# A graph layer on one core: two steps of twelve gathered chunks in place of four of seven, with completion counters of their own

## The chip, the core and the metric

The kernel runs on one core of a Trainium2 chip. The metric is device time in microseconds (us) of one execution. Fourteen runs of the kernel before have a median of 15300.56 us (15264.44 to 15319.17).

## The reference

A graph has 50,000 nodes with a row of 128 float32 each, and 1,650,000 edges, sorted by destination. An edge has a source, a destination and one of two types. Cut to what matters:

```python
Xs = X[src]
m_data = Xs @ W_data.T + b_data
m_ctrl = Xs @ W_control.T + b_control
msg = jnp.where((edge_types == 0)[:, None], m_data, m_ctrl)
agg = jax.ops.segment_sum(msg, dst, num_segments=X.shape[0])
out = jax.nn.relu(agg + (X @ W_self.T + b_self))
return _layernorm(X + out)
```

Every node has one edge to itself, so 50,000 of the edges are loops.

## The kernel before

The two products with the message weights are linear, so the kernel first sums the source rows per destination and type, and multiplies the sums afterwards. The edge list is cut into blocks: `NBLK` = 435, of which 433 are regular and the first and last are plain. A regular block covers 3,800 edges: `Q` = 4 steps of `R` = 7 chunks of 128 edges, 4 x 22 fillers, and 128 single rows.

**Gathers.** For each of the 28 chunks POOL issues one indirect DMA (line 451) that brings 128 source rows of 512 bytes into a tile `y`, out of a pool of 70. TensorE multiplies it with a one-hot matrix `oh` (line 454) whose columns are the 2 x 38 pairs of type and destination in the step's window. The result `acc` of a step is added by VectorE (DVE) into the block's running sums (`add`, line 465), at a place read into a register.

**Loops and fillers.** A loop edge needs no gather, since a node's own row is near. `fill` (lines 297 to 327) takes the loops out of the chunks, puts fillers (other edges) in their places, and works out which nodes were left out. That is a chain of DVE operations on [128, 28, 22] elements: `m`, `new`, `v_new`, `idx`, `col`, `old`, `by`. It runs `RAHEAD` = 5 blocks ahead. The nodes left out come back through `pl` (lines 344 to 358), which `add_left_out` (line 363) adds to the sums.

**Single rows.** The last 128 edges of a block are fetched by ordinary DMAs of one row each, 64 on SP's queue and 64 on ACT's (`single_rows`, line 439), two blocks ahead (`AHEAD`). In each of the four steps either engine loads 16 addresses into registers with one load (line 434) and issues 16 rows. They form a 29th chunk `yx` of the last step.

**Completion.** The tile framework gives each DMA one of a few completion counters, in turn: eight for POOL's gathers, eight shared by the queues of SP and ACT. Whoever issues on a counter first waits until the DMA before on the same counter has landed. In the built program each gather from the ninth on waits for the gather eight before, and once the 70 buffers are used also for TensorE; and almost every single row waits for an earlier transfer.

**Order.** Instructions go to each engine in the order of the loop from line 520 on (`manual_schedule`). Per block: the last step's `add` of the block before; ACT copies the shifted sums over (`take_over`, line 470); DVE adds the left-out nodes; then for each step `products`, and between them the layer of the block before (`layer`, `moments`, `store`, lines 472 to 498), the one-hot and its column counts two blocks ahead (`onehot` line 396, `counts` lines 406 and 411), `fill`, and `single_rows`. SP also carries the loads of a block's own rows (`window`, lines 387 and 389), the output (line 498) and, every ten blocks, the edge lists. Every ten blocks `columns` (lines 234 to 285) prepares the next ten on DVE.

Of the kernel before, what the change touches and what calls it, by code (L numbers as in the profile page):

```python
# [12 lines left out]
BF16 = mybir.dt.bfloat16  # L13
I32 = mybir.dt.int32
U8 = mybir.dt.uint8
# [8 lines left out]
D = 128  # L24
# [9 lines left out]
R = 7  # L34
W = 38
Q = 4
B = 128
C = R * Q
X = 128
C1 = C + 1  # L40
F = 22
# [9 lines left out]
AHEAD = 2  # L51
RAHEAD = 5
LOOP = 1024.0
# [26 lines left out]
def straight(ctx, tc, c, x, x_t, src_t, dst_t, etype_t, src_f, dst_f, etype_f, src_x, dst_first, first_p, out):  # L80
# [19 lines left out]
    gat = ctx.enter_context(tc.tile_pool(name="gat", bufs=70))  # L100
# [9 lines left out]
    idx0 = keep.tile([P, C], I32, name="idx0")  # L110
    nc.sync.dma_start(idx0, src_t[:, :C])
# [5 lines left out]
    FILL = Q * F + C  # L117
# [108 lines left out]
    def packed(src, col, name):  # L226

        lim = eds.tile(list(col.shape), F32, name="lim" + name, bufs=1)
        nc.vector.tensor_scalar(lim, col, 0.0, float(P - 1), op0=ALU.max, op1=ALU.min)
        v = eds.tile(list(col.shape), F32, name="v" + name)  # L230
        nc.vector.scalar_tensor_tensor(v, src, float(P), lim, op0=ALU.mult, op1=ALU.add)
        return v

    def columns(g):
# [5 lines left out]
        def first_of(rel, d):  # L240
            yield (rel[:, :, :C].rearrange(steps, r=R), d[:, :, :C].rearrange(steps, r=R),
                   first[:, :, :, None].to_broadcast([P, GB, Q, R]))
            yield rel[:, :, C:], d[:, :, C:], first[:, :, Q - 1:]

        def first_of_f(rel, d):
# [4 lines left out]
        h = eds.tile([P, GB, Q, R + 1], BF16, name="h_loop", bufs=1)  # L250
        nc.vector.memset(h, 0.0)
        nc.vector.tensor_tensor(h[:, :, :, :R], a["s"][:, :, :C].rearrange(steps, r=R),
                                a["d"][:, :, :C].rearrange(steps, r=R), op=ALU.is_equal)
        rank = ps_r.tile([P, GB * Q, R + 1], F32, name="rank")
        hs_ = h.rearrange("p b q r -> p (b q) r")
        nc.tensor.matmul(rank, below, hs_, start=True, stop=False)
        for r in range(R):
# [10 lines left out]
        cb = eds.tile([P, GB, C], F32, name="cb")  # L268
        nc.vector.tensor_scalar(cb, a["t"][:, :, :C], 0.0, float(P), op0=ALU.not_equal, op1=ALU.mult)
        nc.vector.tensor_tensor(cb, cb, a["d"][:, :, :C], op=ALU.add)  # L270
        nc.vector.tensor_tensor(cb, cb, base[:, g * GB:(g + 1) * GB, :].to_broadcast([P, GB, C]), op=ALU.subtract)


        rk = eds.tile([P, GB, C], F32, name="rk")
        nc.vector.scalar_tensor_tensor(rk.rearrange(steps, r=R), h[:, :, :, :R], -LOOP,
                                       rank.rearrange("p (b q) r -> p b q r", q=Q)[:, :, :, :R],
                                       op0=ALU.mult, op1=ALU.add)
# [3 lines left out]
        stay = eds.tile([P, GB, C], F32, name="stay")  # L281
        nc.vector.scalar_tensor_tensor(stay, rk, F - LOOP, v[:, :, :C], op0=ALU.is_ge, op1=ALU.mult)
# [14 lines left out]
    def fill(b):  # L297

        if plain(b):
# [6 lines left out]
        m = fil.tile([P, C, F], F32, name="m")  # L306
        nc.vector.tensor_tensor(m, rk_g[g][:, i, :, None].to_broadcast([P, C, F]),  # L307
                                rank_no_ps[:, None, :].to_broadcast([P, C, F]), op=ALU.is_equal)
        new = fil.tile([P, C, F], F32, name="new")
        nc.vector.tensor_tensor(new.rearrange("p (q r) f -> p q r f", r=R), m.rearrange("p (q r) f -> p q r f", r=R),  # L310
                                vf.rearrange("p (q f) -> p q f", f=F)[:, :, None, :].to_broadcast([P, Q, R, F]),
                                op=ALU.mult)
        v = fil.tile([P, C], F32, name="v_new")
        nc.vector.tensor_reduce(v, new, AX.X, ALU.add)  # L314
        vi = fil.tile([P, C], I32, name="vi")
        nc.vector.tensor_tensor(vi, v, stay_g[g][:, i, :], op=ALU.add)
        idx = fil.tile([P, C], I32, name="idx", bufs=RAHEAD + 2)
        nc.vector.tensor_single_scalar(idx, vi, 7, op=ALU.logical_shift_right)
        nc.vector.scalar_tensor_tensor(col_g[g][:, i, :C], idx, -float(P), vi, op0=ALU.mult, op1=ALU.add)
        idxs[b] = idx  # L320

        old = fil.tile([P, C, F], F32, name="old")
        nc.vector.tensor_tensor(old, m, cb[:, :, None].to_broadcast([P, C, F]), op=ALU.mult)
        by = fil.tile([P, Q, F], BF16, name="by")
        with nc.allow_low_precision(reason="whole numbers below 256, one of them not 0"):
            nc.vector.tensor_reduce(by, old.rearrange("p (q r) f -> p q f r", r=R), AX.X, ALU.add)  # L326
# [33 lines left out]
    def add_left_out(b):  # L360
        if not plain(b):
            part = sums[b % RING][:, :, :B]
            nc.vector.tensor_tensor(part, pls.pop(b)[:, :, :B], part, op=ALU.add)  # L363

    def chunks_of(b, q):

        n = C1 if not plain(b) else C if b == 0 else RCH if b < NBLK else 0
        return range(q * R, max(q * R, min((q + 1) * R if q < Q - 1 else C1, n)))

    def steps_of(b):  # L370
        return [q for q in range(Q) if len(chunks_of(b, q))]

    idxs = {0: idx0}
    bys, pcs, zs, pls = {}, {}, {}, {}
    ats = {}
    ohs, cnts, ys, accs, xws, xTs, pos, hs, mvs, sds = {}, {}, {}, {}, {}, {}, {}, {}, {}, {}
# [5 lines left out]
    def window(b):  # L384
        at = base_of(b)
        xw = stp.tile([B, D], F32, name="xw", bufs=5)
        nc.sync.dma_start(xw, x[bass.ds(at, B), :])
        xT = stp.tile([P, B], F32, name="xT", bufs=5)
        nc.sync.dma_start(xT, x_t[:, bass.ds(at, B)])
        xws[b], xTs[b] = xw, xT  # L390

    def onehot(b):
        g, i = divmod(b, GB)
        n = C1 if not plain(b) else C if b == 0 else RCH
        oh = ohp.tile([P, C1, 2 * W], F32, name="oh")
        nc.vector.tensor_tensor(oh[:, :n, :], col_g[g][:, i, :n, None].to_broadcast([P, n, 2 * W]),  # L396
                                num_ps[:, None, :].to_broadcast([P, n, 2 * W]), op=ALU.is_equal)
        ohs[b] = oh

    def counts(b):  # L400

        cnt = ohp.tile([P, Q, 2 * W], BF16, name="cnt")
        with nc.allow_low_precision(reason="whole numbers up to R + 1"):
            whole = [q for q in range(Q) if len(chunks_of(b, q)) == R]
            n = len(whole)
            nc.vector.tensor_reduce(cnt[:, :n, :], ohs[b][:, :n * R, :].rearrange("p (q r) w -> p q w r", r=R),  # L406
                                    AX.X, ALU.add)
            for q in steps_of(b):
                if q not in whole:
                    k = chunks_of(b, q)  # L410
                    nc.vector.tensor_reduce(cnt[:, q, :], ohs[b][:, k[0]:k[-1] + 1, :].rearrange("p r w -> p w r"),  # L411
                                            AX.X, ALU.add)
        cnts[b] = cnt

    SHARE = X // 2
    TURN = SHARE // Q
    RANGE = dict(min_val=0, max_val=(N - 1) * ROW, skip_runtime_bounds_check_because="where a node's row is")
    x_bytes = x.rearrange("n d -> (n d)").bitcast(U8)[None, :]

# [7 lines left out]
    def single_rows(b, q):  # L427

        if q == 0:
            ys[b] = stp.tile([X, D], F32, name="yx", bufs=AHEAD + 2)  # L430
        both = []
        for j, (eng, dma) in enumerate(((SP, nc.sync), (ACT, nc.scalar))):
            at = j * SHARE + q * TURN
            _, rows = nc.values_load_multi_w_load_instructions(  # L434
                ats[b][0:1, at:at + TURN], engines=[eng], **RANGE)
            both.append([(dma, at + k, row) for k, row in enumerate(rows)])
        for pair in zip(*both):
            for dma, k, row in pair:
                dma.dma_start(ys[b][k:k + 1, :].bitcast(U8), x_bytes[:, bass.ds(row, ROW)])  # L439

    def products(b, q):
        g, i = divmod(b, GB)
        acc = ps.tile([P, 3, W], F32, name="acc")
        ks = chunks_of(b, q)
        for k in ks:
            if k == C:
                r, y = X, ys.pop(b)
            else:
                r = LAST if b == NBLK - 1 and k == RCH - 1 else P
                y = gat.tile([P, D], F32, name="y")  # L450
                nc.gpsimd.indirect_dma_start(  # L451
                    out=y[:r], out_offset=None, in_=x,
                    in_offset=bass.IndirectOffsetOnAxis(ap=idxs[b][:r, k:k + 1], axis=0))
            nc.tensor.matmul(acc[:, :2, :].rearrange("p t w -> p (t w)"), y[:r], ohs[b][:r, k, :],  # L454
                             start=k == ks[0], stop=k == ks[-1])
        for t in range(2):
            nc.tensor.matmul(acc[:, 2, :], to_row[:, t, :], cnts[b][:, q, t * W:(t + 1) * W],  # L457
                             start=t == 0, stop=t == 1)
        accs[b, q] = acc
# [7 lines left out]
    def take_over(b):  # L467
        at = nc.values_load(shift_i[0:1, b:b + 1], engines=[ACT], min_val=0, max_val=B,  # L468
                            skip_runtime_bounds_check_because="it was clamped to this")
        nc.scalar.copy(sums[b % RING][:, :, :B], sums[(b - 1) % RING][:, :, bass.ds(at, B)])  # L470
# [10 lines left out]
    def moments(b):  # L481
# [5 lines left out]
        nc.vector.bn_aggr(mv, st)  # L487
        sd = stp.tile([B, 1], F32, name="sd")
        nc.scalar.activation(sd, mv[:, 1:2], AF.Sqrt, bias=c["eps"][:B, :])
        hs[b], mvs[b], sds[b] = h, mv, sd  # L490

    def store(b):
# [5 lines left out]
        nc.sync.dma_start(out[bass.ds(base_of(b), B), :], o)  # L498
# [10 lines left out]
    for b in range(1, RAHEAD):  # L509
# [3 lines left out]
        if b < AHEAD:  # L513
            onehot(b)
            counts(b)
            for q in range(Q):
                single_rows(b, q)
        if b == 1:
            clear_sums()
    for b in range(NBLK + 1):  # L520
# [9 lines left out]
        if b > 0:  # L530
            add(b - 1, steps_of(b - 1)[-1])
            if b < NBLK:
                take_over(b)
        if b < NBLK:
            add_left_out(b)
# [393 lines left out]
```

## Time and profile before

| What | Value |
|---|---|
| median of 14 runs | 15300.56 us |
| the profiled execution: its time, and its span | 15289.41 us, 15287.4 us |
| PE busy | 7318.0 us (48%) |
| DVE busy | 6912.4 us (45%) |
| ACT busy | 353.8 us (2%) |
| POOL busy | 11491.8 us (75%) |
| granted TensorE clock | 1.000 |
| mean share of the 16 DMA engines, and rate | 2 tenths, 63 GB/s |
| DMA issues: gathers, single rows | 12160, 2 x 27712 |

The span runs from the first to the last instruction. Busy time of an engine leaves out the instructions of its sequencer: register loads, semaphore waits and the issue of DMAs on SP and ACT. So ACT, busy for 2%, may still have a full queue. For POOL a gather does count as busy[...]. A row of the groups of instructions gives the count, the busy time and the mean of one, then the engine's idle time just before, and what ended it.

### The profile page before, as it was taken

What the parts mean: (1) busy time and instruction counts of PE and PEld (TensorE: products, weight loads), DVE (VectorE), ACT (ScalarE), POOL (GpSimd) and SP (SyncE); (2) the same over time, 40 slices, a digit from 0 to 9 for tenths busy, and PEclk for the clock granted to TensorE, in tenths of its full rate; (3) what the DMA queues carried; (4) which work ended last, traced back from release to release, by engine and by line L of the source; (5) the groups of instructions that cost most, each with busy time, mean ns of one, the idle gap of its engine ahead of it and who ended that gap; (6) DMA issues with size and microseconds to landing.
All of it is one profiled execution on the core that took longest, in us unless ns stands there. A gap on an engine that the chain in (4) does not pass through costs nothing.

```text
span 15287.4 us, 239078 instructions
## 1 busy us (share of the span) xinstructions
PE 7318.0 (48%) x34233; PEld 6788.6 (44%) x34234; DVE 6912.4 (45%) x12861; ACT 353.8 (2%) x875; POOL 11491.8 (75%) x12170
## 2 busy tenths in 40 slices
PE   4444444444444444445666544444444444444444
PEld 3444444444444444444444444444444444444444
DVE  5444444444444444444444444444444444444443
ACT  0000000000000000000000000000000000000000
POOL 7777777777777777777777777777777777777776
DMA  2222222222222222222222222222222222222221
GB/s 66 63 65 63 63 64 65 63 64 63 63 63 65 63 63 63 65 64 64 63 63 63 64 63 63 63 63 64 63 63 63 63 63 63 63 65 63 63 63 52
DMA packets 724493, 968.72 MB, mean 63 GB/s; under 512 B 282786, under 2 KB 522533, under 8 KB 722896
## 3 DMA queue, kind: packets, MB, share of 16 engines
q0 software_dynamic: 389120, 797.69, 20.0%
q1 hardware_dynamic: 277914, 141.12, 3.4%
q10 hardware_dynamic: 55862, 14.50, 0.4%
q14 instruction: 1314, 10.76, 0.2%
q8 instruction: 283, 4.64, 0.1%
HBM read 923.55 MB, written 28.66 MB: 62 GB/s over the span
## 4 chain that ended last, share of the span: by engine, by line
DMA 42%; ACTq 20%; issue 13%; SPq 10%; PE 8%; DVE 6%; ACT 1%; POOL 0%; DVEq 0%; POOLq 0%
DMA yx<-in_x 34%; ACTq L439 16%; SPq L439 8%; PE acc L454 6%; ACTq L434 3%; DMA y<-in_x,idx 3%; DMA out<-o 2%; DMA xT<-in_x_t 2%; DVE sums L363 1%; ACT sums L470 1%; ACTq L468 1%; DMA xw<-in_x 1%; SPq L381 1%; DMA vf_all<-vd 1%; PE pl L349 1%
## 5 line engine op out<-in xcount | busy, mean ns | idle before, releaser
L451 POOL DMA_INDIRECT y<-in_x,idx x12152 | 11482.7, 945 | 3714.7 <-issue 2017.6
L454 PE MATMUL acc<-oh,y 128*128 128x76 f32 x24320 | 5779.5, 424 | 500.2 <-DMA y<-in_x,idx 492.2
L454 PEld LDWEIGHTS acc<-oh,y 128*128 128x128 f32 x24320 | 5431.4, 330 | 691.3 <-DMA y<-in_x,idx 657.1
L363 DVE TENSOR_TENSOR sums<-pl,sums 128x384 f32<-128x384 f32 x433 | 241.3, 557 | 7740.1 <-ACT sums L470 7740.1
L349 PE MATMUL pl<-z,ones_b 88*128 88x256 bf16 x433 | 170.7, 394 | 4403.4 <-DVE sums L363 4265.9
L349 PEld LDWEIGHTS <-ones_b 88*128 88x128 bf16 x433 | 45.2, 104 | 4452.0 <-DVE sums L363 4451.9
L333 PE MATMUL small<-ones_b,by 128*88 128x1 bf16 x433 | 100.2, 232 | 2812.8 <-DVE by L326 2755.7
L333 PEld LDWEIGHTS <-by 128*88 128x88 bf16 x433 | 64.3, 148 | 2860.6 <-DVE by L326 2860.5
L406 DVE TENSOR_REDUCE cnt<-oh 128x228 bf16<-128x1596 f32 (+2 forms) x435 | 1279.0, 2940 | 0.1
L396 DVE TENSOR_TENSOR oh<-col,small 128x2204 f32<-128x2204 f32 (+2 forms) x435 | 1050.0, 2414 | 0.0
L457 PEld LDWEIGHTS <-to_row 128*128 128x128 bf16 x3476 | 633.3, 194 | 0.0
L326 DVE TENSOR_REDUCE by<-old 128x88 bf16<-128x616 f32 x433 | 577.7, 1334 | 15.0
L470 ACT COPY sums<-sums 128x384 f32 x434 | 222.2, 512 | 14139.0 <-DMA yx<-in_x 13648.5
L478 PE MATMUL po<-wmsgT,sums 128*128 128x128 f32 x1740 | 531.5, 461 | 0.0
L465 DVE TENSOR_TENSOR sums<-acc,sums 128x114 f32 x1738 | 473.9, 273 | 126.3 <-PE acc L457 39.0
L411 DVE TENSOR_REDUCE cnt<-oh 128x76 bf16<-128x608 f32 x434 | 503.6, 1160 | 0.0
L457 PE MATMUL acc<-cnt,to_row 128*128 128x38 bf16 x3476 | 473.6, 220 | 0.0
L478 PEld LDWEIGHTS po<-wmsgT,sums 128*128 128x128 f32 x1740 | 403.3, 322 | 97.5 <-issue 97.5
L310 DVE TENSOR_TENSOR new<-m,small 128x616 f32<-128x616 f32 x433 | 344.3, 795 | 14.8
L307 DVE TENSOR_TENSOR m<-rk,small 128x616 f32<-128x616 f32 x433 | 344.3, 795 | 14.7
L314 DVE TENSOR_REDUCE v_new<-new 128x28 f32<-128x616 f32 x433 | 344.1, 795 | 14.8
L476 PE MATMUL po<-bias,sums 3*128 3x128 f32 x870 | 344.5, 497 | 1.2 <-DVE sums L465 1.2
(116 smaller groups left out, 4068.3 us busy)
## 6 DMA issues: line engine op xcount, KB each, us to landing
yx<-in_x ACTq DMA_DIRECT2D x27712, 0.5 KB
yx<-in_x SPq DMA_DIRECT2D x27712, 0.5 KB
y<-in_x,idx POOLq DMA_INDIRECT x12152
xw<-in_x SPq DMA_DIRECT2D x435, 64.0 KB
xT<-in_x_t SPq DMA_DIRECT2D x435, 64.0 KB
out<-o SPq DMA_DIRECT2D x435, 64.0 KB
vf_all<-vd SPq DMA_DIRECT2D x44, 440.0 KB
s<-in_src_t SPq DMA_DIRECT2D x44, 145.0 KB
```

What stands on the lines that cost most here:

```text
L326: nc.vector.tensor_reduce(by, old.rearrange("p (q r) f -> p q f r", r=R), AX.X, ALU.add)
L363: nc.vector.tensor_tensor(part, pls.pop(b)[:, :, :B], part, op=ALU.add)
L396: nc.vector.tensor_tensor(oh[:, :n, :], col_g[g][:, i, :n, None].to_broadcast([P, n, 2 * W]), num_ps[:, None, :].to_broadcast([P, n, 2 * W ...
L406: nc.vector.tensor_reduce(cnt[:, :n, :], ohs[b][:, :n * R, :].rearrange("p (q r) w -> p q w r", r=R), AX.X, ALU.add)
L411: nc.vector.tensor_reduce(cnt[:, q, :], ohs[b][:, k[0]:k[-1] + 1, :].rearrange("p r w -> p w r"), AX.X, ALU.add)
L434: _, rows = nc.values_load_multi_w_load_instructions(ats[b][0:1, at:at + TURN], engines=[eng], **RANGE)
L439: dma.dma_start(ys[b][k:k + 1, :].bitcast(U8), x_bytes[:, bass.ds(row, ROW)])
L451: nc.gpsimd.indirect_dma_start(out=y[:r], out_offset=None, in_=x, in_offset=bass.IndirectOffsetOnAxis(ap=idxs[b][:r, k:k + 1], axis=0))
L454: nc.tensor.matmul(acc[:, :2, :].rearrange("p t w -> p (t w)"), y[:r], ohs[b][:r, k, :], start=k == ks[0], stop=k == ks[-1])
L457: nc.tensor.matmul(acc[:, 2, :], to_row[:, t, :], cnts[b][:, q, t * W:(t + 1) * W], start=t == 0, stop=t == 1)
L465: nc.vector.tensor_tensor(part, accs.pop((b, q)), part, op=ALU.add)
L478: nc.tensor.matmul(po, a[:, t, :B], c["wmsgT"][:, t * D:(t + 1) * D], start=False, stop=t == 1)
```

## The change

- A step has `R` = 12 chunks and `W` = 60 destinations, a block `Q` = 2 steps, 2 x 42 fillers and 2 x 64 single rows: 3,284 edges, 24 gathers, 128 single rows. `NBLK` is 503. A block's sums have `B` = 112 columns.
- The 64 single rows of a step are a 13th chunk of 64 partitions in each step. `fill`, `columns` and `counts` run over `C1` = 26 chunk columns in place of 28 or 29, with 42 fillers.
- Gathers go in passes of 6 into one tile of 6 x 128 rows, of which there are `SLOTS` = 10. Each slot has a semaphore `landed`; the six gathers of a pass count on it, and TensorE waits once for all six. The framework's counters and their waits are gone from the gathers.
- Single rows count on semaphores `fetched`, one for each queue and each of four buffers. TensorE waits once a block for all 128. The framework's waits between rows are gone. An engine loads 32 addresses at a time, twice a block.
- `take_over` on ACT and `add_left_out` on DVE become one DVE operation, `begin_sums`. The square root stands in a function of its own (`root`), a pass later, and `store` a pass later than before.

```diff
-R = 7
-W = 38
-Q = 4
-B = 128
+R = 12
+W = 60
+Q = 2
+PASS = 6
+B = 112
 C = R * Q
-X = 128
-C1 = C + 1
-F = 22
+F = 42
+S = 64
+X = Q * S
+R1 = R + 1
+C1 = Q * R1
...
+SLOTS = 10
...
-    gat = ctx.enter_context(tc.tile_pool(name="gat", bufs=70))
+    gat = ctx.enter_context(tc.tile_pool(name="gat", bufs=SLOTS))
...
+        with nc.allow_low_precision(reason="whole numbers up to R1"):
+            nc.vector.tensor_reduce(cnt, ohs[b].rearrange("p (q r) w -> p q w r", r=R1), AX.X, ALU.add)
...
         for j, (eng, dma) in enumerate(((SP, nc.sync), (ACT, nc.scalar))):
-            at = j * SHARE + q * TURN
+            at = j * TURN + part * LOAD
             _, rows = nc.values_load_multi_w_load_instructions(
-                ats[b][0:1, at:at + TURN], engines=[eng], **RANGE)
...
-                dma.dma_start(ys[b][k:k + 1, :].bitcast(U8), x_bytes[:, bass.ds(row, ROW)])
...
+            for dma, sem, k, row in pair:
+                copy = dma.dma_start(ys[b][k:k + 1, q, :].bitcast(U8), x_bytes[:, bass.ds(row, ROW)])
+                copy.then_inc(sem, 16)
+                tc.no_tile_sem_insts.add(copy.ins.name)
+                tc.add_to_no_dep_group(f"single{b}", copy.ins)
+
+    def rows_fetched(b):
+
+        times = len(range(b % ROW_SLOTS or ROW_SLOTS, b + 1, ROW_SLOTS))
+        for j in range(2):
+            wait = nc.tensor.wait_ge(fetched[j][b % ROW_SLOTS], 16 * Q * TURN * times)
+        tc.declare_fence(wait.ins, group=f"single{b}")
...
+    def gathers(b, ks):
+        i = pass_no[0] % SLOTS
+        pass_no[0] += 1
+        y = gat.tile([P, PASS, D], F32, name="y")
         for k in ks:
...
+            r = LAST if b == NBLK - 1 and k == RCH - 1 else P
+            copy = nc.gpsimd.indirect_dma_start(
+                out=y[:r, k % PASS, :], out_offset=None, in_=x,
+                in_offset=bass.IndirectOffsetOnAxis(ap=idxs[b][:r, column(k):column(k) + 1], axis=0))
+            copy.then_inc(landed[i], 16)
+            tc.no_tile_sem_insts.add(copy.ins.name)
+            tc.add_to_no_dep_group(f"rows{b}_{ks[0]}", copy.ins)
+        seen[i] += 16 * len(ks)
+        wait = nc.tensor.wait_ge(landed[i], seen[i])
+        tc.declare_fence(wait.ins, group=f"rows{b}_{ks[0]}")
+        return y
...
+    def begin_sums(b):
+
+        part = sums[b % RING][:, :, :B]
+        if b == 0:
+            return
+        at = nc.values_load(shift_i[0:1, b:b + 1], engines=[DVE], min_val=0, max_val=B,
                             skip_runtime_bounds_check_because="it was clamped to this")
-        nc.scalar.copy(sums[b % RING][:, :, :B], sums[(b - 1) % RING][:, :, bass.ds(at, B)])
+        old = sums[(b - 1) % RING][:, :, bass.ds(at, B)]
+        if plain(b):
+            nc.vector.tensor_copy(part, old)
+        else:
+            nc.vector.tensor_tensor(part, pls.pop(b)[:, :, :B], old, op=ALU.add)
...
         if b > 0:
             add(b - 1, steps_of(b - 1)[-1])
-            if b < NBLK:
-                take_over(b)
         if b < NBLK:
-            add_left_out(b)
...
+            begin_sums(b)
+        last = steps_of(b)[-1:]
+        for q, (step, ks) in enumerate(passes_of(b)):
+            if ks:
+                products(b, step, ks)
...
             if q == 1 and b > 0:
+                root(b - 1)
+            if q == 2 and b > 0:
                 store(b - 1)
...
-            if not plain(b + AHEAD):
-                single_rows(b + AHEAD, q)
+            if q % 2 == 0 and not plain(b + AHEAD):
+                single_rows(b + AHEAD, q // 2, 0)
```

## The prediction

> **What bounds the kernel now.** I first read the engines' busy shares and the costliest group, then POOL's waits, then single gathers in the timeline, then the queues of SP and ACT, and last the end of the span. The page:
>
> ```profile
> span 15287.4 us, 239078 instructions
> ...
> L451 POOL DMA_INDIRECT y<-in_x,idx x12152 | 11482.7, 945 | 3714.7 <-issue 2017.6
> ```
>
> POOL's busy share of 75% misleads. A gather costs its 945 ns and the idle time before it: (11482.7 + 3714.7) / 12152 = 1.2506 us. All 12160 gathers take 15207 us, 99.5% of the span. Is the idle part a wait? POOL's waits (total us, times, longest) and the first gathers of the timeline answer:
>
> ```profile
> POOL y L451 <- issue: 2018.8, 6615, 0.3
> POOL y L451 <- PE acc L454: 890.8, 2901, 2.4
> POOL y L451 <- DMA y<-in_x,idx: 453.9, 1486, 0.3
> ```
>
> ```profile
> 9.66 0.94 POOL L451 DMA_INDIRECT y<-in_x,idx  x1 [0.31 <-issue]
> 10.91 0.94 POOL L451 DMA_INDIRECT y<-in_x,idx  x1 [0.30 <-issue]
> 12.16 0.94 POOL L451 DMA_INDIRECT y<-in_x,idx  x1 [0.30 <-issue]
> ```
>
> Whatever is named as the releaser, the gap is 0.30 us (890.8 / 2901 = 0.307). In the built program the second to eighth gather wait for nothing, neither a counter nor a buffer, and they too start 1.25 us apart. So the gap belongs to the gather, and POOL waits for nobody: the kernel is bound by the count of gathers at 1.2506 us each. A regular block has 28, so 35.0 us.
>
> Close behind comes the issue of single rows. ACT's copy (line 470) starts at 5019.50 and 5054.49, again 35.0 us apart, and DVE waits for that copy 7740.1 us in all. A stretch of the chain of waits on ACT (start, length):
>
> ```profile
> 5003.49 1.36 ACTq L434
> ...
> 5005.88 0.23 ACTq L439
> ...
> 5006.22 0.23 ACTq L439
> ...
> 5006.55 0.23 ACTq L439
> ...
> 5007.55 1.62 DMA yx<-in_x
> ```
>
> Free rows start 0.333 us apart; then the queue stands 1.62 us until an earlier row has landed and its counter is free. SP has the same waits:
>
> ```profile
> SPq L439 <- DMA yx<-in_x: 1880.0, 4977, 1.8
> L434 ACTq TENSOR_LOAD <-at_x x1732: 1010/1299/1499, 23.9 to 15228.0; - x193
> L434 SPq TENSOR_LOAD <-at_x x1732: 972/1225/1462, 36.8 to 15223.0; - x193
> ```
>
> That is 1880.0 / 433 = 4.3 us a block on SP, and a load of 16 addresses costs 1.2 to 1.3 us.
>
> At the end POOL's last gather starts at 15214.04, takes 0.99, and the span goes on for 72 us: the copies on ACT and the products are about two blocks behind POOL. The first gather starts at 8.2. So 8.2 + 15207 + 72 = 15287.
>
> **The change, part by part.**
>
> *Gathers.* The built program has 24 + 501 x 24 + 13 = 12061 in place of 12160: 99 x 1.2506 = 124 us less, on the path. The framework's counters go, but as shown they hold nobody up: 0. In their place POOL waits once in six gathers, for TensorE to be done with the pass ten before, 75 us earlier. Behind that wait stand all later gathers. I take 0, as long as the other engines keep to 24 x 1.2506 = 30.0 us a block. That is the condition of the whole forecast, so each engine is summed against 30.0.
>
> *SP.* 64 rows. One costs issue 228 ns, a register move 29 and gaps of about 70, 0.327 us as on ACT: 20.9. Loads of 32 addresses do not occur in the trace. One address costs 0.540 us (line 381), 16 cost 1.225, so 46 ns for each more and 1.96 for 32; bounds are 1.225 (no more than for 16) and 2.45 (twice it). I take 1.96, from two rows of the same form; with 0.1 around each, 4.1 for both. Window and output: one load 0.54, three DMAs of 0.36, 0.36 and 0.38, gaps 0.4: 2.0. Nine issues per ten blocks for the edge lists at 0.45: 0.4. Sum 27.4, between 26.0 and 28.4. The output waits for DVE's `store`, and the second 32 rows are queued behind it; TensorE needs these only two blocks later, so the wait must only leave SP its 27.4 between one `store` and the next.
>
> *ACT.* 64 x 0.333 = 21.3; two loads of 2.08 (0.569 for one address on line 468, 1.299 for 16) and 0.3 for the slower first row after each: 4.8; the root 0.3 and its wait about 0.2. Sum 26.6. The copy of 0.51 and its load of 0.57 leave ACT.
>
> *The waits on rows.* The 4.3 us a block on SP, and some 6 on ACT (35.0 less 26.6 and the copy), go. Do they come back because the transfers are slow? The Trainium skill (DMA: Bandwidth & Descriptors, "Why a DMA increments its semaphore by 16 and not by 1") says that a DMA of one row from SP or ACT runs on the lowest-numbered engine alone, which speaks against this change: 128 rows in 30.0 us on one of 16. The table of queues gives ACT's rows 0.4% of 16 engines' span: 0.004 x 16 x 15287 / 27712 = 35 ns each. By the rule 128 x 35 ns = 4.5 us, with the gathers' 20% beside them about 11 of 30.0; spread evenly it would be 6. Either way there is room. I take 0.
>
> *DVE.* Elementwise operations grow by 1.04 ns an element (2418 ns at 2204, 755 at 608). `m`, `new`, `v_new`, `old` at 26 x 42 = 1092 elements: 795 + 476 x 1.04 = 1290 each, 5.16 us; `oh` at 3120: 3.37. For the column counts three rows give the law:
>
> ```profile
> L411 DVE TENSOR_REDUCE cnt<-oh 128x76 bf16<-128x608 f32 x433 | 503.4, 1163 | 0.0
> L406 DVE TENSOR_REDUCE cnt<-oh 128x304 bf16<-128x2128 f32 x1 | 3.9, 3856 | 0.0
> L406 DVE TENSOR_REDUCE cnt<-oh 128x76 bf16<-128x532 f32 x1 | 1.1, 1078 | 0.0
> ```
>
> With 7 elements an output costs (3856 - 1078) / 228 = 12.2 ns, over a base of 150; an eighth adds 85 / 76 = 1.1. So 13 cost 18.9, times 240 outputs: 4.7 us; by elements alone it would be 5.6. `by`, likewise, 1.84 to 2.25. Two `add` of 0.34, `begin_sums` 0.51, the other small rows of a block unchanged at 3.5, `columns` 7.8 per ten blocks 0.8, three register loads of 0.30 that are partly covered 0.9. Sum 21.5, at most 22.8, against 15.9 busy before. DVE now waits 7740.1 / 433 = 17.9 us a block for ACT's copy; that goes, and next it waits for TensorE's layer after the first pass, within the 8.5 us left over.
>
> *PE.* 26 products of two records each. 14 records of 76 columns take 3.2 us, 0.23 each; line 478 with 128 columns takes 0.30. So at most 52 x 0.30 = 15.6, plus layer 2.8 and small ones 2: 20.4. The wait for six gathers makes the first of them late by 6.3 us; nothing but the order on TensorE hangs on that, and `add` needs the last of a step anyway.
>
> *DVE against POOL.* The Trainium skill (SBUF — State Buffer, "SBUF: two separate sides") warns that while DVE runs certain copies from SBUF to SBUF, POOL cannot write descriptors. The candidates here, `o`, `idx` and `at_x` (0.374 + 0.218 + 0.243 = 0.84 us a block), would by the rule cost up to 433 x 0.84 = 364 us now and 420 after. The row says otherwise: a mean of 945 against 0.94 in the timeline, 12 us in all. I scale that by 503 / 435: +2.
>
> *The tail.* ACT no longer lags. From the last gather: landing about 2 (a row took 1.62), one product and the counts 1.2, `add` 0.8, layer 2.8, moments and root 1.4, `store` 0.6, then the last checks on DVE 2.9 and 13.4 from DVE's end at 15274.0 to the span's: 25. The trace has no such drain; bounds are 20 and the present 72. I take 27, nearer to the sum.
>
> **Sum.** 8.2 + 12061 x 1.2506 + 2 + 27 = 15121. The profiled execution is 2.0 over its span, and the median of the runs is 11.2 over it: 15121 + 13 = 15134 us, 1.1% under 15300.56.
>
> **The rivals.**
>
> *The rows' waits were the queue's own (slower).* If SP or ACT cannot issue 32 rows in a run at 0.33 us, and the 4.3 us come back in another form, SP takes 27.4 + 4.3 = 31.7 a block, POOL stands at its slots, and 501 x 31.7 + 37 before the first row + 60 after the last + 13 gives 15990. It decides from 2.6 us a block on: 40 ns a row, or 1.3 us a load. For it: 32 rows in a run are nowhere in the trace, and SP has 9% of slack. Against it: seven free rows in the chain follow each other without slowing, and a row takes 35 ns of a DMA engine. 9%.
>
> *DVE, or the loop between DVE and TensorE, exceeds 30.0 at times.* `columns` adds 7.8 us in one block of ten; with 8.5 to spare and 60 gathers in buffers I expect no stall. If the spare were 2 and POOL stood 6 us in each of 51 groups: 15134 + 306 = 15440; at half of it 15290. 4%.
>
> *The counters do pace POOL (much faster).* If half the 0.30 were the wait on a counter: 12061 x 1.10 + 48 = 13320. The unwaited gathers speak against it. 3%.
>
> **How the numbers follow.** POOL-bound at the same pace has 84%, and its time is the prediction. Its own range: 10 less at the undisturbed pace of 1.2498, 7 less tail, 11 less if the next median lies at the profile; 45 more with today's tail, 20 more for twice the disturbance: 15095 to 15215. That holds over 8 in 10 and needs no other case. A measurement of this kernel can tell about 0.2% (30 us) from no change. Faster: 84 + 3 = 87%; same: 3 of the DVE case's 4; slower: 9 + 1.
>
> **What would show it.** Right: the gather row at 945 ns with 1.25 us a gather and 12061 of them; no wait of POOL over 0.3 us in the middle of the span; rows on SP and ACT 0.33 us apart without waits; DVE near 70% busy; a tail under 40 us. Wrong: POOL waiting for TensorE for microseconds once a pass, with SP or ACT never idle (first rival) or DVE never idle (second); loads of 32 addresses over 3 us; gathers clearly over 0.95 us.

## The result, and the profile after

The changed kernel takes 15122.34 us (median of 6 runs, 15121.93 to 15125.28) against 15300.28 us for the kernel before (28 runs): ratio 0.9884, interval 0.9874 to 0.9894. The forecast was 15134 us. The profiled execution takes 15124.06 us. But in two of the three later groups of runs, each on a chip of its own, the kernel before took 45% longer and the changed kernel 57 to 59%, so that there the change made the kernel 7.5 to 8.6% slower.

From the page of the changed kernel, its span and three of its groups (busy us, mean ns of one | idle time before):

```profile
span 15122.4 us, 243274 instructions
...
L464 POOL DMA_INDIRECT y<-in_x,idx x12048 | 11393.6, 946 | 3681.9 <-issue 3577.2
...
L409 DVE TENSOR_REDUCE cnt<-oh 128x240 bf16<-128x3120 f32 x503 | 2914.8, 5795 | 0.1
L525 DVE SCALAR_TENSOR_TENSOR h<-po,xw 112x128 f32<-112x128 f32 x503 | 146.6, 291 | 2996.3 <-PE po L520 2942.6
```

A gather costs (11393.6 + 3681.9) / 12048 = 1.2513 us, as before to a thousandth. There are 12061 of them (13 stand in a row of their own). The first starts at 8.6, the last at 15098.7; it takes 1.0, and the span goes on for 22.6 us after its end, where it went on for 72 before. Of the 165 us between the two spans the gathers make up 115 and this tail 50. POOL's waits (total us, times, longest):

```profile
POOL y L464 <- issue: 3581.2, 11733, 0.3
...
POOL y L464 <- PE acc L483: 14.8, 39, 3.2
```

No wait of weight is left, though POOL now has one wait per pass. The condition of the forecast was that the other engines keep to 30.0 us a block. The new loads of 32 addresses (minimum/median/maximum ns), then the wait of SP that is largest in total:

```profile
L435 ACTq TENSOR_LOAD <-at_x x1002: 2121/2154/2474, 21.0 to 15009.8; - x167
L435 SPq TENSOR_LOAD <-at_x x1002: 1866/2077/2257, 33.0 to 15021.1; - x167
```

```profile
SPq L543 <- DVE o L542: 730.9, 335, 27.5
```

All waits of SP together are 1353 us over the whole span, and 2.5 us a block between 1000 and 14000 us: SP works 27.5 of each 30.0 us. ACT's queue, counted in the same way from the trace, works 24.9 and waits 5.1, nearly all for DVE. The waits of a row for an earlier row (1880.0 us before) are gone. DVE is busy 10619.7 us (70%), 21.1 a block, and its largest idle time is the one for TensorE's layer (line 525), 5.9 us a block.

### The profile page after: what moved, and what is told of

Read it like the earlier page. It is cut to its first block, busy times and chain, and to the rows that moved or that the text cites. A ratio compares the mean times of both kernels' runs of the same rounds, so it can differ in the third digit from the quotient of the medians.

```text
span 15122.4 us, 243274 instructions
## 1 busy us (share of the span) xinstructions
PE 8027.3 (53%) x34836; PEld 6859.4 (45%) x34837; DVE 10619.7 (70%) x13316; ACT 151.6 (1%) x509; POOL 11407.5 (75%) x12071
## 3 DMA queue, kind: packets, MB, share of 16 engines
q10 hardware_dynamic: 64566, 16.74, 0.6%
## 4 chain that ended last, share of the span: by engine, by line
POOL 59%; issue 21%; PE 9%; DMA 6%; DVE 5%; PEld 1%; SPq 0%; ACTq 0%; POOLq 0%; PEldq 0%; ACT 0%; DVEq 0%
POOL y L464 59%; DMA y<-in_x,idx 5%; PE acc L483 5%; PE po L520 2%; PE po L518 1%; DVE cnt L409 1%; PE po L517 1%; DVE by L329 0%; PEld acc L483 0%; DVE h L525 0%; SPq L440 0%; DVE st L527 0%; ACTq L440 0%; DVE m L310 0%; DVE new L313 0%
## 5 line engine op out<-in xcount | busy, mean ns | idle before, releaser
L464 POOL DMA_INDIRECT y<-in_x,idx x12048 | 11393.6, 946 | 3681.9 <-issue 3577.2
L483 PE MATMUL acc<-oh,y 128*128 128x120 f32 x24122 | 5749.8, 427 | 6309.0 <-PEq L471 6281.6
L409 DVE TENSOR_REDUCE cnt<-oh 128x240 bf16<-128x3120 f32 x503 | 2914.8, 5795 | 0.1
L401 DVE TENSOR_TENSOR oh<-col,small 128x3120 f32<-128x3120 f32 x503 | 1695.8, 3371 | 0.0
L329 DVE TENSOR_REDUCE by<-old 128x84 bf16<-128x1092 f32 x501 | 1066.9, 2130 | 17.4
L489 PE MATMUL acc<-oh,yx 64*128 64x120 f32 x2004 | 767.3, 484 | 8.2 <-PEq L449 8.2
L310 DVE TENSOR_TENSOR m<-rk,small 128x1092 f32<-128x1092 f32 x501 | 647.1, 1292 | 17.1
L313 DVE TENSOR_TENSOR new<-m,small 128x1092 f32<-128x1092 f32 x501 | 647.0, 1291 | 17.0
L317 DVE TENSOR_REDUCE v_new<-new 128x26 f32<-128x1092 f32 x501 | 646.7, 1291 | 17.0
L326 DVE TENSOR_TENSOR old<-m,small 128x1092 f32<-128x1092 f32 x501 | 642.9, 1283 | 0.0
L520 PE MATMUL po<-wmsgT,sums 128*112 128x128 f32 x2012 | 518.7, 403 | 0.0
```

Source lines behind the costliest of these rows:

```text
L401: nc.vector.tensor_tensor(oh, col_g[g][:, i, :, None].to_broadcast([P, C1, 2 * W]), num_ps[:, None, :].to_broadcast([P, C1, 2 * W]), op=AL ...
L409: nc.vector.tensor_reduce(cnt, ohs[b].rearrange("p (q r) w -> p q w r", r=R1), AX.X, ALU.add)
L464: copy = nc.gpsimd.indirect_dma_start(out=y[:r, k % PASS, :], out_offset=None, in_=x, in_offset=bass.IndirectOffsetOnAxis(ap=idxs[b][:r, c ...
L520: nc.tensor.matmul(po, a[:, t, :B], c["wmsgT"][:, t * D:(t + 1) * D], start=False, stop=t == 1)
```

## The experiments

### First group: what the counters and the loads are worth (kernel before: 15270.07 us)

**Rows back on the shared counters.** Only the single rows lose their own semaphores; the layout and the gathers stay as changed.

```diff
-                copy = dma.dma_start(ys[b][k:k + 1, q, :].bitcast(U8), x_bytes[:, bass.ds(row, ROW)])
-                copy.then_inc(sem, 16)
...
+                dma.dma_start(ys[b][k:k + 1, q, :].bitcast(U8), x_bytes[:, bass.ds(row, ROW)])
```

> The changed kernel with the single rows back on the framework's shared counters, so that a row again waits for an earlier transfer; gathers keep their own. Theory (POOL is bound by the count of its gathers, and the own counters of the rows only let SP and ACT fit under 30.0 us a block): the 4.3 us a block that SP stood before come back, SP takes some 31.9, POOL waits for TensorE once a pass, time 15,600 to 16,200, about 16,050. Rival (fewer gathers alone made the gain, the rows' waits are hidden): 15,122.

Measured: 16778.41 us, ratio 1.0987 (1.0965 to 1.1009). The waits of POOL, of SP's queue and of DVE for ACT's root (line 529):

```profile
POOL y L461 <- PE acc L480: 1729.8, 482, 7.4
```

```profile
SPq L440 <- DMA yx<-in_x: 2067.2, 7722, 2.3
```

```profile
DVE rstd L535 <- ACT sd L529: 4049.6, 501, 19.6
```

SP stands 4.1 us a block for earlier rows, and POOL stands 3.6 us about once a block for a slot. So without own counters for the rows the layout with two steps loses 10%. The time lies above the expected range: a block takes (16765 - 100) / 501 = 33.3 us. SP's 27.5 + 4.1 = 31.6 does not explain that. Counted from the trace between 1000 and 14000 us, SP's queue waits 4.6 us a block in all and takes 28.7 for the rest, 1.2 more than in the changed kernel; ACT's waits 6.9, of which 6.0 are for earlier transfers, and takes 26.4. So both queues are full, 33.3 us a block each. That DVE waits for ACT's root shows that ACT's queue is late; but the two queues share the eight counters, each may wait for a row of the other, and no run shows which of them sets the pace.

**Gathers back on the shared counters.**

```diff
-            copy = nc.gpsimd.indirect_dma_start(
+            nc.gpsimd.indirect_dma_start(
...
-        seen[i] += 16 * len(ks)
-        wait = nc.tensor.wait_ge(landed[i], seen[i])
```

> The changed kernel with the gathers back on the framework's eight counters in turn, each gather waiting for the one eight before; rows keep their own counters. Theory: the gather's own 0.30 us hides that wait, 1.251 us a gather, 15,122 within 15 us. Rival (the counters pace POOL): 15,240 to 15,300, with a longer gap before each gather.

Measured: 15166.26 us, ratio 0.9932 (0.9915 to 0.9948), 44 us over the changed kernel's median, where at most 15 were expected. The profiled span is 15135.0, 12.6 us over. POOL's waits:

```profile
POOL y L464 <- issue: 3281.0, 10739, 1.5
POOL y L464 <- DMA y<-in_x,idx: 198.3, 600, 2.2
```

198.3 / 600 = 0.33 us is the gap that every gather has, under another name; the same reading as in the prediction. All gathers together are 1.2522 us apart, 0.001 more than in the changed kernel (11 us in all); most of that lies between 287 and 438 us from the start, where 29 gathers stand 1.4 to 3.1 us apart. So by the spans the counters of the gathers are worth next to nothing, as predicted; the 44 us between the medians are taken up with the next run.

**The sums copied by ACT again**, DVE adding the left-out nodes afterwards.

```diff
-        if plain(b):
-            nc.vector.tensor_copy(part, old)
-        else:
-            nc.vector.tensor_tensor(part, pls.pop(b)[:, :, :B], old, op=ALU.add)
+        nc.scalar.copy(part, sums[(b - 1) % RING][:, :, bass.ds(at, B)])
+        if not plain(b):
+            nc.vector.tensor_tensor(part, pls.pop(b)[:, :, :B], part, op=ALU.add)
```

> The changed kernel with the taking over of the sums back on ACT (a copy) and a separate addition of the left-out nodes on DVE. Theory: ACT has about 4 us of 30.0 to spare and the copy with its register load costs 1.1, so 15,120 to 15,150. Rival (DVE's taking over was what removed the lag): DVE waits for a copy queued behind 64 rows, POOL stands, 15,250 or more.

Measured: 15148.94 us, ratio 0.9921 (0.9904 to 0.9937); profiled span 15117.9, 4.5 us below the changed kernel's, with gathers 1.2509 apart. DVE does wait for ACT again:

```profile
DVE sums L510 <- ACT sums L508: 451.4, 501, 4.2
```

0.9 us a block in place of 17.9, with room to spare. The ratios of this kernel and of the one with shared counters lie 0.4 and 0.5% above that of the changed kernel, though their spans lie 4.5 us below and 12.6 above its. Two things make this up: in this group the kernel before takes 15270.07 us, 30 less than beside the changed kernel, and the first execution of every kernel, here the profiled one, is 23 to 44 us shorter than the others, for a reason that no run shows. The changed kernel itself was not run in this group, so ratios and medians of the two groups can't be set against each other to better than some 50 us. Within the group the kernel with shared counters takes 17 us more than this one, by the medians and by the spans. So a copy on ACT by itself does not hold DVE up; what did so before is then most likely ACT's queue of rows ahead of the copy.

**Loads of 8 addresses**, eight on each queue a block in place of two of 32.

```diff
-    LOAD = TURN // 1
+    LOAD = TURN // 4
...
-                for part in range(1):
+                for part in range(4):
...
```

> The changed kernel with eight loads of 8 addresses a block on either queue in place of two of 32. Theory (SP needs about 27.6 of 30.0 us, ACT about 26): 3.3 more on SP and 4.9 more on ACT bring both to about 30.9, 15,400 to 15,800, about 15,590. Rival (the queues have much more to spare than the sum says): 15,122.

Measured: 15476.08 us, ratio 1.0134 (1.0114 to 1.0155), within the range.

```profile
L435 ACTq TENSOR_LOAD <-at_x x4008: 717/827/1128, 20.7 to 15380.6; - x191
L435 SPq TENSOR_LOAD <-at_x x4008: 526/782/1066, 32.8 to 15417.8; - x191
```

Eight loads of 0.78 cost 6.3 us where two of 2.08 cost 4.2; with the gaps around six more loads SP comes to (15452 - 100) / 501 = 30.6 us a block and waits for 164 us in all. This shows the edge of the forecast: 3 us more a block on SP (and more on ACT too), and POOL waits (313.0 us for TensorE in 151 places). It also shows that an address is cheap and a load dear: (2077 - 782) / 24 = 54 ns for each address from the ninth on, against 782 for the first eight.

### Second group: the same change on another chip (kernel before: 22190.35 us)

This group, meant for small differences, ran where the kernel before took 45% longer. The first two kernels are the changed kernel unaltered and the one with the gathers on shared counters.

> The changed kernel itself, run beside the next three on one chip, so that they can be compared with it. All theories: 0.9884 of the kernel before, within 0.001; 12061 gathers 1.251 us apart and a tail of 20 to 25 us.

> The same kernel as e2, beside the changed one. Theory (the wait of a gather for the one eight before is hidden): the time of e5 within 10 us. Rival (the shared counters do hold POOL now and then: e2's mean distance of two gathers was 1.2522 us against 1.2513): 10 to 40 us over e5.

Measured: 24093.17 us, ratio 1.0857 (1.0841 to 1.0872), and 24138.75 us, ratio 1.088 (1.0865 to 1.0895). That is 46 us more, outside both expected ranges and on the side of the rival; but POOL is not the bound here, as the waits below show, so it says little about the normal run.

The third puts only the single rows of the kernel before on counters of their own:

```diff
-                dma.dma_start(ys[b][k:k + 1, :].bitcast(U8), x_bytes[:, bass.ds(row, ROW)])
+                copy = dma.dma_start(ys[b][k:k + 1, :].bitcast(U8), x_bytes[:, bass.ds(row, ROW)])
+                copy.then_inc(sem, 16)
...
+            wait = nc.tensor.wait_ge(fetched[j][b % ROW_SLOTS], 16 * SHARE * times)
```

> The kernel before with one part of the change alone: the single rows count on semaphores of their own and do not wait for each other; blocks, gathers, loads of 16 and ACT's copy as before. Theory (12160 gathers at 1.251 us set the pace, and ACT's lag sets the tail): the pace stays, the tail falls from 72 to 25 to 40 us, so 30 to 50 us less than before, ratio 0.997. Rival (the rows' waits held the kernel back and freeing them is most of the gain): ratio 0.989. Third (neither): 1.000.

Measured: 22157.32 us, ratio 0.9988 (0.9973 to 1.0002). The fourth has 68 single rows a step, 32 on SP and 36 on ACT in two loads of 18, and 12032 gathers:

```diff
-S = 64
+S = 68
...
-    TURN = S // 2
-    LOAD = TURN // 1
+    SHARES = ((0, 32), (32, 36))
```

> The changed kernel with 68 single rows in a step, 32 on SP and 36 on ACT (in two loads of 18), so 3,292 edges in a block and 12032 gathers. Theory (POOL-bound, ACT at some 29.4 of 30.0 us): 29 x 1.251 = 36 us under e5, ratio 0.986. Rival (ACT passes 30.0 or its root comes late for DVE): at or over e5, ratio 0.988 or more.

Measured: 24984.62 us, ratio 1.1262 (1.1246 to 1.1278). The expectations were made for a chip on which the kernel before takes about 15,300 us. None had in view what happened here, and what they were to tell apart stays undecided: above all, whether counters of their own for the rows, without fewer gathers, would have gained anything where the kernel before takes 15,300 us. What was slow? The gathers of the changed kernel in this group, and POOL's largest wait:

```profile
L464 POOL DMA_INDIRECT y<-in_x,idx x12048 | 11376.3, 944 | 12617.5 <-PE acc L483 7775.5
```

The gather itself is unchanged at 944 ns, and so are DVE's operations (the column counts take 5834 ns). The transfers are no slower: the gathers' queue has 11.5% of 16 engines' span, 0.115 x 24107 = 2770 us, against 0.208 x 15122 = 3150 in the normal run. POOL stands because slots do not come free. The chain of waits, which the profile can follow here for only about a third of the span, has SP's rows (line 440) as its largest share, 17%; and SP's queue waits for others only 0.9 us of 48.0 a block (from 1000 to 14000 us). The instructions of that line on SP, first in the normal run of the changed kernel, then in this one (minimum/median/maximum ns):

```profile
L440 SPq MOVE yx<-in_x x32064: 29/29/37, 34.9 to 15033.3; - x200
```

```profile
L440 SPq MOVE yx<-in_x x32064: 1/29/2112, 42.1 to 24076.4; - x200
```

A register move never takes over 37 ns in the one and up to 2.1 us in the other. The raw records of SP's queue (start in us, duration in ns) show the form:

```
7011.528    13  DMA_DIRECT2D
7011.544     3  MOVE
7011.576   718  DMA_DIRECT2D
7012.308     3  MOVE
7012.315    12  DMA_DIRECT2D
...
7015.329   691  MOVE
7016.034     4  DMA_DIRECT2D
7016.051   699  MOVE
```

The queue stands for about 0.70 us, in an instruction or between two, does one to four instructions in a burst, and stands again. Counting stands of 0.55 to 0.9 us, SP has some 17,000 in the whole run with 12,000 us, ACT 11,000 with 7,700; the normal run has 11 and 4. SP stands in 50% of the span, ACT in 32%, both together in 26%, where 16% would be chance. And they stand beside gathers: rows that SP issues within 1.3 us of the start of a gather are 0.99 us apart on average, those issued over 3 us after the last gather's start 0.42 (median 0.32). In the normal run nearly all rows lie beside gathers and are 0.40 apart on average (distances up to 5 us, loads among them). So in this group the rows of SP are slow while POOL issues gathers; ACT's are 0.81 apart beside gathers and 0.39 in pauses.

### Third group: is it the issue of rows? (kernel before: 22129.38 us)

Another chip, and the same slowness. Beside the changed kernel once more:

> The changed kernel unaltered, as the reference of this group. Where the kernel before takes about 15,270 to 15,300 us: 15,120 to 15,160, and gathers 1.25 us apart. Where it takes about 22,200 us, as in the second group: 24,100 (23,900 to 24,300), with SP and ACT standing in steps of 0.70 us while POOL issues gathers and not while POOL pauses. Rival for the second case (those stops have another cause, and came and went with the group): the time is then nowhere near either.

Measured: 23782.04 us, ratio 1.0751 (1.0733 to 1.0769): some 120 us under the expected range, but the same slowness, with SP's rows 0.98 us apart beside gathers and 0.42 in pauses.

**23 gathers**, and **20 gathers**, in place of 24 in a regular block. These kernels leave out the gathers and their products, so the sums lack those rows:

```diff
+def OUT(b, k):
+    return not plain(b) and k == 20
...
+            if OUT(b, k):
+                continue
```

For 20, the condition is `k % PASS == 4`.

> Leaves out one gather and its product in each of the 501 regular blocks (23 in place of 24). Theory, POOL's count of gathers sets the time: 501 x 1.2513 = 627 us less than the changed kernel beside it (600 to 650). Rival, SP is already the bound at 27.6 us a block or nearly so: less than 400 us less, and POOL waits for TensorE. Where the kernel before takes 22,200 us: the row queues are the bound, a gather less frees them for 1.25 us, and the time falls by 200 to 600 us only.

> Leaves out four gathers and their products in each of the 501 regular blocks (20 in place of 24, 25.0 us of gathers). If POOL stayed the bound: 501 x 4 x 1.2513 = 2508 us less, 12,620. By the sums for the engines SP with 27.6 us a block is late first: 501 x 27.6 + 100 = 13,930 (13,750 to 14,300), POOL waiting for TensorE once a pass, SP never idle, ACT at 26.6 close behind, DVE at 21.1 not the bound. If DVE or TensorE with the loop between them were next: over 14,500. Where the kernel before takes 22,200 us: about 22,700 (22,000 to 23,500).

Measured: 23126.06 us, ratio 1.0453 (1.0436 to 1.0471), and 21451.69 us, ratio 0.9696 (0.968 to 0.9712). Both fall more than expected (656 us, not 200 to 600; 2330, not about 1400). I had let rows go on during a gather at a third of their speed, so that a gather less would save only part of its 1.25 us. By the spans the first gather left out saves (23713.5 - 23041.8) / 501 = 1.34 us a block, and four save (23713.5 - 21356.0) / (501 x 4) = 1.18 us each, about all of their time. What these two were meant for, SP's floor at about 27.5 us a block, could not be seen here and stays untested.

**Half the row issues**, the same bytes:

```diff
-                ats[b][0:1, q * S + at:q * S + at + LOAD], engines=[eng], **RANGE)
+                ats[b][0:1, q * S + at:q * S + at + LOAD - MANY], engines=[eng], **RANGE)
...
+        for j, dma in enumerate((nc.sync, nc.scalar)):
+            k = (j + 1) * TURN - MANY
+            copy = dma.dma_start(ys[b][k:k + MANY, q, :], x[k:k + MANY, :])
```

> Changes what is fetched: of each queue's 32 single rows a step only 16 are fetched one by one, the other 16 places are filled by one transfer of 16 neighbouring rows of x, which are not the rows wanted. 34 issues in place of 64 on each of SP and ACT for a block; the bytes are the same. Where the kernel before takes about 15,300 us: the row queues are not the bound, so the time of the changed kernel beside it within 20 us, with SP idle for some 10 us a block. Where it takes 22,200 us, theory (the issue of rows is what is slow there, beside gathers): 16,500 (15,100 to 18,000), 7,000 us less than the changed kernel. Rival there (the slowness sits in the gathers or in the products): less than 1,000 us less.

Measured: 17799.17 us, ratio 0.8043 (0.8028 to 0.8058), 5983 us less than the changed kernel beside it, within the range; the rival (under 1,000) is out. By the spans an issue less on each queue saves (23713.5 - 17804.7) / (501 x 30) = 0.393 us, loads included. SP, now with 34 issues a block, still stands beside gathers. POOL's idle time falls by half, first the changed kernel of this group, then this one:

```profile
L464 POOL DMA_INDIRECT y<-in_x,idx x12048 | 11406.7, 947 | 12193.5 <-PE acc L483 7440.7
```

```profile
L471 POOL DMA_INDIRECT y<-in_x,idx x12048 | 11380.8, 945 | 6345.6 <-issue 3301.6
```

**What follows.** In the third group each gather left out saves about 1.18 us, and each row issue less on both queues 0.39. These are prices of a change, not of the whole: all gathers and rows of the changed kernel at these prices make 12061 x 1.18 + 32064 x 0.393 = 26830 us, 3050 more than measured, and those of the kernel before are 3110 over, so that some of the work does go on side by side. By these prices the change, which swaps 99 gathers for 32064 - 27712 = 4352 more rows on each queue, costs 4352 x 0.393 - 99 x 1.18 = 1590 us. Measured: 1653 in this group, 1903 in the second. The kernel with 68 rows a step fits roughly: 64 rows fewer on SP and 3936 more on ACT, 1936 more on the mean of the two, cost 1936 x 0.393 = 761 us, less 34 for 29 gathers, so 727; measured 891 over the changed kernel beside it. Why gathers hold up the other queues here and not in the first group is not settled. No run shows a cause, only that the gathers themselves and DVE keep their speed and that the transfers are no slower; nor is it shown that it belongs to the chip and not to the hour.

## Why the prediction was right, point by point

**POOL bound by the count of gathers: right.** 8.6 + 12061 x 1.2513 + 22.6 = 15123, with a measured span of 15122.4, against 8.2 + 12061 x 1.2506 + 2 + 27 = 15121. That the two agree to 1.4 us is partly luck: the gathers take 6 us more than forecast and the tail 4 less. That the gap of 0.30 us belongs to the gather is shown twice: it is unchanged once the framework's waits are gone, and putting those waits back (first group) costs 0.001 us a gather by the spans. The third rival, counters that pace POOL, is out.

**The term that missed** is the last one, the 11.2 us from the profiled execution to the median. It was carried over from the kernel before; here the median lies 1.7 us below the profiled time. These 12.9 us, less 1.4 by which the span was put too low, are the error of 12 us. The prediction had this as one of its terms downwards (11 less if the median lies at the profile). Its terms make a range of 15106 to 15199, not 15095 to 15215; the measured time lies in both.

**SP: 27.4 predicted, 27.5 measured; ACT: 26.6 predicted, 24.9 measured.** The load of 32 addresses takes 2.08 us, not 1.96 (predicted 46 ns for each further address, measured 54 from 8 to 32), and two of them make up 0.24; the rows, 0.32 us apart in place of 0.327, give most of it back. ACT's loads took 2.15 where 2.08 was put down, within the bounds given for SP's, but its rows were 0.32 apart in place of 0.333, and the sum came out 1.7 too high.

**DVE: 21.5 predicted, 21.1 measured, with one wrong law.** The two are not the same sum: the predicted one holds 0.9 for register loads, which busy time leaves out, so 20.6 stands against 21.1. The column counts take 5.80 us. Of the two laws the prediction took the one by outputs (4.7) and gave the one by elements (5.6) as the other end; the second is nearer: 5795 / 3120 = 1.86 ns an element, where the rows of the kernel before give 1163 / 608 = 1.91 and 3856 / 2128 = 1.81. The 1.1 ns for an eighth element, from one row, did not carry on to thirteen. `m`, `new`, `v_new` and `old` take 1.29 as predicted, `oh` 3.37, `by` 2.13 within its bounds. Smaller sums elsewhere made up for part of the 1.1 us that the counts were over. `columns` causes no stall, so the second rival is out here.

**The stall that goes:** next is late, as predicted, TensorE's layer for DVE, 5.9 us a block, within the spare 8.5. TensorE itself, put at no more than 20.4 us a block, is busy 8027.3 / 503 = 16.0.

**DVE against POOL:** 945.7 ns a gather against 944.9, about 9 us in all, whatever their cause; predicted 2, by the rule (the Trainium skill, SBUF — State Buffer, "SBUF: two separate sides") up to 420. The row decided rightly. For the other rule (the Trainium skill, DMA: Bandwidth & Descriptors, "Why a DMA increments its semaphore by 16 and not by 1") ACT's queue has two packets a row (64566 for 32064 rows), so a row is not spread over 16 engines; which engine it takes no view shows. With 0.6% of 16 engines' span it gives 0.006 x 16 x 15122 / 32064 = 45 ns a row, 128 of them 5.8 us of 30.0: no bound, though by these rounded shares 10 ns more than before.

**The tail: 27 predicted, 22.6 measured.** It was the lag of the row queues that made it 72: with the rows back on the shared counters it is 68.6, with loads of 8 addresses 65.2, with only the copy back on ACT 23.0.

**The first rival, rows that cannot be issued in a run: out in the result and the first group, and true in another form in the other two groups.** In the normal run rows follow at 0.32 us without waits. The rival had 9%, on the grounds that 32 rows in a run are nowhere in the trace. What it could not have from the trace is the other form in which rows can be slow: not through their counters but beside gathers on POOL. And its price of 15990 fits neither case, since it was made from SP's waits alone. Where the counters bring it about (first group), the prediction's own sum for ACT, 26.6 + 6 = 32.6 us, was the larger one, and would have given 501 x 32.6 + 110 = 16443, nearer to the 16778. The range holds where SP and ACT run freely; nothing in the prediction says so, and the one profile that it had could not show it.

## What to carry to other kernels

When one engine is bound by a count of instructions and each costs the same whatever it waits for, the gain of taking some away is the count times that price, and the work of a forecast is to sum every other engine against the new pace; SP had 2.5 us of 30.0 left, and register loads that took 3 us more, gaps included, already cost 2%. Moving work to idle-looking queues is only free while the queues run beside each other: here the same exchange of 99 gathers for 8704 rows, with the rest of the change, gains 1.2% where they do and costs 7.5 to 8.6% where they don't, so a change of this kind is to be timed on several chips. Whether a wait is real is seen from its length, not from its name: the 0.30 us of the gathers stood under three names and was no wait under any.

## What the runs showed of the hardware that was not expected

**Queues that stand beside gathers**, in steps of 0.70 us, in two of the three later groups, as told above. It is the largest effect in the study (22190 against 15300 us for one and the same kernel), and the profile shows where it sits only in the times of the queue's own instructions: a register move of up to 2112 ns.

**A granted clock of 1.000 can mean that there is no record.** The page gives 1.000 for the kernel before and 0.544 after. Lines of the timeline of TensorE (start, us, and the count of records), first from before, then from after, and the granted clock in stretches of after (the number of two digits behind POOL's):

```profile
7024.09 1.22 PE L478 MATMUL po<-wmsgT,sums 128*128 128x128 f32 x4
```

```profile
7009.74 1.60 PE L483 MATMUL acc<-oh,y 128*128 128x120 f32 x12 [2.19 <-PEq L471]
...
7020.42 2.92 PE L483 MATMUL acc<-oh,y 128*128 128x120 f32 x12
...
7024.39 1.20 PE L520 MATMUL po<-wmsgT,sums 128*112 128x128 f32 x4
```

```profile
7008.00:7012.00 4.00, 2.26 (x16) 1.84 (x16) 3.79 (x17) 0.00 (x0) 3.03 (x4) 0.93 0.22 54
...
7020.00:7024.00 4.00, 3.68 (x16) 3.43 (x17) 1.75 (x6) 0.00 (x0) 3.09 (x4) 0.50 0.34 87
7024.00:7028.00 4.00, 4.00 (x18) 3.60 (x17) 2.31 (x4) 0.00 (x0) 3.08 (x4) 0.50 0.24 62
```

After, twelve records take 1.60 us where the granted clock is near 0.93 and 2.92 where it is 0.50. The four records of the layer take 1.20 at 0.50, and 1.22 in the kernel before, whose trace holds no record of a clock at all. Two of these records that follow each other start 109 ns apart after at a recorded clock of 1.0 and 213 at 0.5; before, none of 1305 such distances, from all parts of the span, is under 212. So wherever the layer ran, the kernel before ran at half clock too, and its 1.000 in the table is not a measurement. For the time it made no difference, since POOL, not TensorE, is the bound in both kernels.
